# Digits for the second quarter of q and k, and three groups of transfers moved to SyncE, in a kernel of masked attention with an adjacency product

## The chip, the cores and the metric

The kernel runs on one core of a Trainium2 chip. The metric is device time in microseconds (us) of one execution; lower is better. The engines are named as in the profile: PE is TensorE, DVE is VectorE, ACT is ScalarE, POOL is GpSimd, SP is SyncE.

## What is computed

64 batches of 256 rows of 512 numbers pass two layers. Cut to what matters:

```
q = (x @ Wq + bq).reshape(b, n, 8, 64)          # k and v alike
scores = einsum('bqhd,bkhd->bhqk', q, k) / sqrt(64)
scores = scores + (1.0 - adj) * -1000000000.0
attn = softmax(scores)
out = einsum('bhqk,bkhd->bqhd', attn, v).reshape(b, n, 512) @ Wo + bo
x = layernorm(x + out)
y = einsum('nm,bmd->bnd', adj, x)
x = layernorm(x + y @ weight + bias)
```

## The kernel before

**Digits.** Plain fp32 products are slow on TensorE, so nearly all products are made of three products of shorter numbers (type fp32r). A number is cut into a high part (`split_high`, L118, ScalarE), a rest and a sum of both (`split_rest`, L123 and L124, two VectorE operations), and the rest is scaled (`split_scale`, L127, ScalarE). The names in the profile are high, low and diff (for x of the first pair sh, sl and sd; for weights the three buffers wr). `parts_of` (L334) issues for one block of 128 columns three groups of four matmuls (L339), in the order low, high, diff, or high, low, diff where `operands` (L331) says `soon`.

**Pairs and stages.** The batches are worked in 32 pairs p. A pair needs five sets of weights: qk0 (the first 256 columns of wq and wk), qk1 (the other 256), v, o and l. The list STAGES (L96) gives their order. Six buffers wr of 1 MB hold two stages. In the first pairs a stage is cut from the raw weights by `ring_high`, `ring_rest` and `ring_scale`, and `keep` (L129) stores its digits in DRAM by POOL's queue; later `load_w` (L105) brings them back by POOL's queue when `end_stage` is passed.

**The first pair is special.** The two quarters of q and of k that belong to qk0 (j = 0 and 1) are made in plain fp32 from the raw weights (L321, L322): four blocks, each of four fp32 matmuls that stand as eight rows in the profile. The first pair's first scores are therefore fp32 too. Stage qk0 is cut only later, for the second pair: `high` in `start` at L708 and L709, `rest` and `scale` at L713, after `scores(0, 1)`.

**Order.** `start` (L696), `first` (L646), `second` (L668) and `ending` (L720) write the order of work out by hand for TensorE, VectorE, ScalarE and POOL: within `tc.manual_schedule` (L764) these engines follow the source. SP is not among them: a planner orders its transfers. Each engine works its list in order, so an operation that waits holds all behind it. [...]

**Transfers by SP and POOL near the start.** SP loads x of the first pair, wq and wk in column parts (`load_columns`, L167), adj, wv, x of the second pair (`load_x`, L75, each of four transfers with runs of 128 B), bo and b1, and then x of the third pair as buffers come free. POOL stores the digits and loads wo (`load_o`, L208, called in L705). wo is used by `bv_wo` (L237) and when stage o is cut.

**Buffers that matter here.** Tile pools reuse buffers by name. The four buffers named low first hold x of the first pair and later x's low digits of the second (`x_rest`, L292); the four named diff hold its diff digits. `values` (L398) writes its sums into the one buffer zc (L413) and its products into the two buffers vc (L425), of which adj has one at first.

**The end.** `normed` (L530) normalizes a row block in place. For the last pair it issues the store at once: whole row blocks by SP, the last one in two halves, the first half by ScalarE and the second by SP (L543 to L545).

Of the kernel before, what the change touches and what calls it, by code (L numbers as in the profile page):

```python
# [8 lines left out]
F32 = mybir.dt.float32  # L9
F32R = mybir.dt.float32r  # L10
# [5 lines left out]
P = 128  # L16
# [19 lines left out]
def fast(tc, x, adj, wq, bq, wk, bk, wv, bv, wo, bo, w1, b1, out):  # L36
# [6 lines left out]
    nc = tc.nc  # L43
    B, N, D = x.shape
    HD = D // H
    DC = D // P
    NC = N // P
    NP = B // 2
    HF = D // 2
# [11 lines left out]
    one = pool("one", 1)  # L61
    two = pool("two", 2)
    four = pool("four", 4)
# [4 lines left out]
    banks = pool("banks", 8, space=bass.MemoryType.PSUM)  # L68

    XC, XF, XP, R, Q, K, V, E, SM, O, SET, HL, ST, LN = ({} for _ in range(14))  # L70
    RAW, SCRATCH, W, UNCUT, BEGUN = {}, {}, {}, {}, {}

    def load_x(p, i):  # L75

        if p < NP:

            t = XC[p, i] = two.tile([P, D], F32, name="o" if p == 1 and i > 1 else "x")
            for q in range(4):  # L80
                nc.sync.dma_start(t[q * 32:(q + 1) * 32].rearrange("i (m j) -> i m j", j=32), xb[p, i, q])
# [20 lines left out]
    def ring(name):  # L102
        return [wring.tile([P, 2, 2, D], F32R, name="wr") for _ in range(3)]
# [25 lines left out]
    def keep(name, i, part):  # L129

        SCRATCH[name, i] = scratch.tile([P, 2, 2, D], F32, name=f"{name}{i}")
        nc.gpsimd.dma_start(SCRATCH[name, i], part.bitcast(F32))

    def in_ring(f, name, p, k):

        stage = name, p
        if stage not in W:
            W[stage] = ring(name)
        t = [w[:, k // 2, k % 2] for w in W[stage]]
        if name in "vol":  # L140
            f(RAW[name, k], t)
        else:
            g, which = int(name[2]), "qk"[k // 2]
            raw = RAW[which][:, 2 * (k % 2):2 * (k % 2) + 2, g * HF:(g + 1) * HF]
            f(raw, [u.rearrange("p (k e) -> p k e", k=2) for u in t])
        if k == DC - 1 and f is not split_high:
            for i in (0, 2) if f is split_rest else (1,):
                keep(name, i, W[stage][i])

# [5 lines left out]

    def ring_scale(name, p, k):
        in_ring(split_scale, name, p, k)

# [33 lines left out]
    for k in range(DC):  # L194
        RAW["v", k] = four.tile([P, D], F32, name="high")
        nc.sync.dma_start(RAW["v", k], wv[k * P:(k + 1) * P])
    for i in range(4):
        load_x(1, i)
    bo_s, b1_s = on_all(bo, "bo"), on_all(b1, "b1")

    def small_ones():
# [2 lines left out]
        nc.gpsimd.memset(first_of_32, 0.0)  # L204
        for d in range(DC):
            nc.gpsimd.memset(first_of_32[d * 32:d * 32 + 1], 1.0)

    def load_o(k):  # L208
        if k % 2 == 0:
            RAW["o"] = two.tile([P, 2, D], F32, name="hl")  # L210
        RAW["o", k] = RAW["o"][:, k % 2]
        nc.gpsimd.dma_start(RAW["o", k], wo[k // 2 * HF:(k // 2 + 1) * HF].rearrange("(h a i) e -> a h i e", h=4, a=2)[k % 2])

    def load_l():
        t = two.tile([P, DC, D], F32, name="r")
# [98 lines left out]
    def operands(name, p, j, k):  # L314

        cols = slice(j * P, (j + 1) * P)
        if name == "v":
            pairs = [(XP[p, k][i][:, cols], W["v", p][i][:, k // 2, k % 2]) for i in range(3)]
        elif name in "qk":
            g, c = divmod(j, 2)  # L320
            if p == 0 and g == 0:  # L321
                return [(RAW[name][:, k, cols], XF[p, k])]  # L322
            e = slice(c * P, (c + 1) * P)
            w = [t[:, "qk".index(name)].rearrange("p s (k e) -> p (s k) e", k=2)[:, k, e] for t in W[f"qk{g}", p]]
            pairs = [(w[i], XP[p, k][i]) for i in range(3)]
        else:
            b, c = divmod(j, 2)
            t = SET[name, p, b, k // 2]
            pairs = [(t[i][:, k % 2, c * P:(c + 1) * P], W[name, min(p, NP - 2)][i][:, k // 2, k % 2]) for i in range(3)]

        soon = p == 1 and name in "qk" and j == 0 or p == NP - 1 and name in "ol"  # L331
        return [pairs[i] for i in ((0, 1, 2) if soon else (1, 0, 2))]

    def parts_of(pm, name, p, j, of=(0, 3)):  # L334
# [12 lines left out]
    def product(name, p, j):  # L347
        if (name, p, j) in BEGUN:
            pm = BEGUN.pop((name, p, j))
            n = parts_of(pm, name, p, j, (1, 3))  # L350
        else:
            pm = banks.tile([P, D], F32, name="ps")
            n = parts_of(pm, name, p, j)
        scale = RHO if n == 3 else 1.0
        b, c = divmod(j, 2)
        if name in "ol":
            r = R[p][b][:, c]
            if c == 0:
                ST[p, name, b] = two.tile([P, 2], F32, name="sums")
            nc.vector.scalar_tensor_tensor(r, pm, scale, r, op0=OP.mult, op1=OP.add, accum_out=ST[p, name, b][:, c:c + 1])  # L360
        elif name == "v":
            if c == 0:
                V[p, b] = two.tile([P, NC, D], F32, name="v")
            nc.scalar.activation(V[p, b][:, c], pm, AF.Copy, scale=scale)
        else:
            T, bias = (K, bk_s) if name == "k" else (Q, bq_s)
            if c == 0:
                T[p, b] = one.tile([P, 2, 3, D], F32R if n == 3 else F32, name=name + "T")
            if n == 3:
                to = UNCUT[name, p, j] = two.tile([P, D], F32, name="uncut")  # L370
            else:
                to = T[p, b][:, c, 0]
            nc.scalar.activation(to, pm, AF.Identity, bias=bias[:, j:j + 1], scale=scale)  # L373
# [112 lines left out]
    def masks(p, g, b):  # L486
        return [(masked, p, g, b, 0), (masked, p, g, b, 1), *([(summed, p, g, b)] if (p, g) != (NP - 1, 1) else [])]
# [145 lines left out]
    def do(*tasks):  # L633
        for t in tasks:
            for f, *args in (t if isinstance(t, list) else [t]):
                f(*args)
# [54 lines left out]
    def steps_of(*args):  # L691

        h, r, s = ([(f, *args, k) for k in range(4)] for f in (ring_high, ring_rest, ring_scale))
        return h[:2], r[:1] + h[2:3] + r[1:2] + h[3:], r[2:3] + s[:1] + r[3:] + s[1:2], s[2:]

    def start():  # L696
        make_identity(nc, ident)
        do(*((x_first, i) for i in range(4)), (biases,), *((x_high, 0, i) for i in range(4)), (small_ones,))
        qk1, v = (steps_of(*stage) for stage in STAGES[:2])
        high, rest, scale = ([(f, "qk0", 1, k) for k in range(DC)] for f in (ring_high, ring_rest, ring_scale))  # L700
        do((block, "q", 0, 0), (x_rest, 0, 0), (x_rest, 0, 1), qk1[0], (block, "k", 0, 0), (x_rest, 0, 2), (x_rest, 0, 3),
           qk1[1], (block, "q", 0, 1), qk1[2], v[0], (block, "k", 0, 1), v[1][:1], (x_t, 1, 0),
           (adj_t,), qk1[3])
        scores(0, 0)
        do(v[1][1:], (x_t, 1, 1), masks(0, 0, 0), (block, "q", 0, 2), v[2], *((load_o, k) for k in range(DC)), (qk_high, "q", 0, 2), (qk_rest, "q", 0, 2), v[3], (test_adj,),  # L705
           (block, "k", 0, 2), (x_high, 1, 0), (x_high, 1, 1), (qk_high, "k", 0, 2), (qk_rest, "k", 0, 2), masks(0, 0, 1),
           (block, "q", 0, 3), (k_low, 0, 2), (qk_high, "q", 0, 3), (qk_rest, "q", 0, 3), (x_rest, 1, 0), (x_t, 1, 2),
           (block, "k", 0, 3), (stage_end, 0), (qk_high, "k", 0, 3), (qk_rest, "k", 0, 3), (x_rest, 1, 1), (x_t, 1, 3), high[:2],  # L708
           (block, "v", 0, 0), (x_high, 1, 2), high[2:], (k_low, 0, 3), (block, "v", 0, 1), (x_rest, 1, 2),  # L709
           (block, "v", 0, 2), (x_high, 1, 3), (x_rest, 1, 3), (block, "v", 0, 3), (stage_end, 0), (load_r, 0), (load_l,))  # L710
        values(0, 0)
        scores(0, 1)
        do((bv_wo,), rest[:2], scale[:1], rest[2:3], scale[1:2], rest[3:], scale[2:])  # L713
        qk0 = [(f, name, 1, j) for j in range(2) for name in "qk" for f in (qk_high, qk_rest)]
        m = masks(0, 1, 0) + masks(0, 1, 1)
        do((begun, "q", 1, 0), (begun, "k", 1, 0), (block, "q", 1, 0), m[:4], qk0[:2], (block, "k", 1, 0), m[4:5], qk0[2:4], m[5:],
           (block, "q", 1, 1), (k_low, 1, 0), qk0[4:6], (o_high, 0, 0, 0), (o_high, 0, 1, 0), (o_rest, 0, 0, 0),
           (with_bv,), (block, "k", 1, 1), qk0[6:], (stage_end, 0), (k_low, 1, 1), (o_rest, 0, 1, 0))
# [42 lines left out]
           (last_variance,), (root, 1), (less, p, "l", 1, c1), (normed, p, "l", 3, D // 2))  # L761

    PE, DVE, ACT, POOL = mybir.EngineType.PE, mybir.EngineType.DVE, mybir.EngineType.Activation, mybir.EngineType.Pool
    with tc.manual_schedule(engines={PE, DVE, ACT, POOL}):  # L764
        start()
        first(1, steps_of("o", 0))
        second(1)
        load_r(1)
        for w in range(2, NP - 1):
            first(w)  # L770
            second(w)
        ending()

    good = one.tile([P, 2, N // 32], F32, name="z")
# [186 lines left out]
```

## Time and profile before

| what | before |
|---|---|
| median of 3 runs | 2391.67 us (2391.25 to 2391.77) |
| the profiled execution: device time | 2391.06 us |
| its span (first to last instruction) | 2389.2 us |
| granted TensorE clock, mean | 0.999 |
| PE / DVE / ACT / POOL busy | 2374.3 / 1991.0 / 1505.4 / 443.5 us |
| DMA moved | 608.70 MB, mean 255 GB/s |
| PE busy from 8 to 22 us (x of first pair, q and k in fp32) | 13.92 us |
| PE busy from 69 to 77 us | 7.54 us |
| DMA share from 37 to 48 us | 1.09 of the 16 engines |

The page gives busy time by engine, the granted clock and DMA share in 40 slices, the chain that ended last and the costliest groups. A row of the timeline has start, length, engine, line, operation and tiles, output before input. A TensorE row's end is modelled, so durations of matmuls are read from one start to the next. The profiled execution has its own time; a sum of rows is made against it and then carried over to the median of the runs.

### The profile page before, as it was taken

How to read it: one execution, taken by the hardware profiler on the slowest of the kernel's cores; microseconds unless marked ns; L12 is line 12 of the kernel's file. 1: busy time of each engine (PE TensorE's matmuls, PEld its weight loads, DVE VectorE, ACT ScalarE, POOL GpSimd, SP SyncE). 2: the span in 40 equal slices, each digit the busy share in tenths (PEclk: the TensorE clock that was granted, in tenths of full speed). 3: DMA queues.
4: the chain of work that ended last, by engine and by line, in shares of the span. 5: the costliest groups of instructions: out<-in, count | busy, mean ns of one | idle time of the engine just before them, and what ended most of it. 6: DMA issues, size and time to landing. Idle time of an engine off the chain costs nothing.

```text
span 2389.2 us, 43002 instructions
## 1 busy us (share of the span) xinstructions
PE 2374.3 (99%) x16925; PEld 1907.5 (80%) x16925; DVE 1991.0 (83%) x3311; ACT 1505.4 (63%) x2793; POOL 443.5 (19%) x755
## 2 busy tenths in 40 slices
PE   9999999999999999999999999999999999999998
PEld 6788887888878888878888788887888878888776
DVE  7988888888888888888988888888888888888867
ACT  6666666566565665666656656666566665666655
POOL 1222111111111111121111112111111111121121
PEclk9999999999999999999999999999999999999999
DMA  9897788777888777887777967788778887777782
GB/s 295 274 310 244 265 255 283 259 230 256 260 265 271 241 237 256 264 293 238 236 255 254 310 240 224 265 255 286 258 227 261 261 264 268 238 244 255 256 274 62
DMA packets 373651, 608.70 MB, mean 255 GB/s; under 512 B 272316, under 2 KB 275908, under 8 KB 313156
## 3 DMA queue, kind: packets, MB, share of 16 engines
q0 software_dynamic: 71632, 500.21, 57.5%
q1 hardware_dynamic: 301104, 105.29, 20.4%
q8 instruction: 135, 2.21, 0.4%
q14 instruction: 72, 0.59, 0.1%
q10 hardware_dynamic: 708, 0.40, 0.1%
HBM read 551.29 MB, written 49.28 MB: 251 GB/s over the span
## 4 chain that ended last, share of the span: by engine, by line
PE 96%; DVE 1%; ACT 0%; issue 0%; POOLq 0%; ACTq 0%
PE ps L339 72%; PE ps L421 9%; PE ps L455 8%; PE ps L615 5%; PE ps L411 3%; DVE e L476 0%; DVE wr L124 0%; DVE wr L123 0%; PE ps L565 0%; DVE kT L389 0%; DVE qT L387 0%; DVE qT L385 0%; ACT kT L394 0%; DVE kT L385 0%; ACT waste L517 0%
## 5 line engine op out<-in xcount | busy, mean ns | idle before, releaser
L373 ACT ACTIVATE uncut<-ps,numbers 128x512 f32<-128x512 f32 x252 | 174.0, 690 | 274.0 <-PE ps L339 218.1
L476 DVE TENSOR_TENSOR e<-e,adjT 128x1024 f32<-128x1024 f32 x252 | 299.3, 1219 | 0.2 <-ACT e L470 0.2
L339 PE MATMUL ps<-low,wr 128*128 128x512 f32 x992 | 271.6, 395 | 0.0
L339 PE MATMUL ps<-wr,sl 128*128 128x512 f32 x1008 | 270.6, 390 | 0.1
L339 PE MATMUL ps<-wr,sh 128*128 128x512 f32 x1008 | 269.8, 389 | 0.0
L339 PE MATMUL ps<-wr,sd 128*128 128x512 f32 x1008 | 269.4, 389 | 0.0
L339 PE MATMUL ps<-high,wr 128*128 128x512 f32 x992 | 266.4, 390 | 0.0
L339 PE MATMUL ps<-diff,wr 128*128 128x512 f32 x992 | 265.0, 389 | 0.0
L523 POOL TENSOR_TENSOR ln<-ln,numbers 128x2 f32<-128x2 f32 x127 | 140.4, 1105 | 667.0 <-DVE ln L522 621.3
L470 ACT ACTIVATE e<-ps 128x512 f32<-128x512 f32 x504 | 253.3, 629 | 8.6 <-PE ps L455 8.6
L517 ACT ACTIVATE waste<-r,ln 128x512 bf16<-128x512 f32 x255 | 184.0, 722 | 104.6 <-DVE ln L510 98.9
L421 PE MATMUL ps<-e,v 128*32 128x256 f32 x4032 | 229.1, 379 | 0.0
L538 ACT ACTIVATE r<-r,ln 128x512 f32<-128x512 f32 x254 | 193.7, 811 | 55.1 <-DMA x<-in_x_dram 29.9
L339 PEld LDWEIGHTS ps<-wr,sh 128*128 128x128 f32 x1008 | 189.3, 188 | 39.9
L339 PEld LDWEIGHTS ps<-wr,sd 128*128 128x128 f32 x1008 | 189.2, 188 | 39.5 <-DMA wr<-o 0.2
L339 PEld LDWEIGHTS ps<-high,wr 128*128 128x128 f32 x992 | 186.2, 188 | 41.9 <-ACT e L470 0.8
L339 PEld LDWEIGHTS ps<-diff,wr 128*128 128x128 f32 x992 | 186.2, 188 | 39.1
L339 PEld LDWEIGHTS ps<-wr,sl 128*128 128x128 f32 x1008 | 186.9, 188 | 38.2 <-issue 0.4
L455 PEld LDWEIGHTS ps<-qT,kT 64*128 64x128 f32 x3056 | 187.8, 187 | 27.1 <-PE ps L421 12.4
L385 DVE SCALAR_TENSOR_TENSOR qT<-qT,uncut 128x512 fp32r<-128x512 f32 x126 | 86.8, 689 | 146.9 <-ACT qT L378 146.8
L339 PEld LDWEIGHTS ps<-low,wr 128*128 128x128 f32 x992 | 177.7, 188 | 35.5 <-ACT wr L127 0.6
L455 PE MATMUL ps<-qT,kT 64*128 64x256 f32 x3056 | 201.6, 285 | 0.5 <-ACT kT L394 0.5
(166 smaller groups left out, 4156.1 us busy)
## 6 DMA issues: line engine op xcount, KB each, us to landing
wr<-qk POOLq DMA_DIRECT2D x183, 1024.0 KB, 7.6
wr<-v POOLq DMA_DIRECT2D x93, 1024.0 KB, 6.8
wr<-o POOLq DMA_DIRECT2D x90, 1024.0 KB, 7.8
wr<-l POOLq DMA_DIRECT2D x90, 1024.0 KB, 8.6
r<-in_x_dram SPq DMA_DIRECT2D x32, 1024.0 KB, 12.0
out_dram<-r SPq DMA_DIRECT2D x62, 512.0 KB, 2.9
x<-in_x_dram SPq DMA_DIRECT2D x488, 64.0 KB, 5.4
qk<-wr POOLq DMA_DIRECT2D x6, 1024.0 KB, 8.3
```

The source lines that it names most:

```text
L339: nc.tensor.matmul(pm, *pairs[k][i], start=i == 0 and k == 0, stop=i == n - 1 and k == DC - 1)
L373: nc.scalar.activation(to, pm, AF.Identity, bias=bias[:, j:j + 1], scale=scale)
L385: nc.vector.scalar_tensor_tensor(low, high.bitcast(F32), -RHO, UNCUT.pop((name, p, j)), op0=OP.mult, op1=OP.add)
L411: nc.tensor.matmul(at[h * 32:(h + 1) * 32, b, :], ones, chunk[h], start=i == 0, stop=i == len(sm) - 1)
L421: nc.tensor.matmul(at[h * 32:(h + 1) * 32, a, :], V[p, b][:, kc, col:col + 32], E[p, g, b, kc][0][h % 2][:, h // 2, :], start=kc == 0, sto ...
L455: nc.tensor.matmul(sc[s][:, a, :], K[p, g][r, a, i, keys], Q[p, g][r, a, i, b * N:(b + 1) * N], start=i == digits[0], stop=i == digits[-1])
L470: nc.scalar.activation(e[s], sc[s], AF.Exp, scale=(RHO if (p, g) != (0, 0) else 1.0) * qscale)
L476: nc.vector.tensor_tensor(e, e, mask[:, kc:kc + 1, :].to_broadcast([P, e.shape[1], N]), op=OP.mult)
L517: nc.scalar.activation(waste, R[p][b][:, c], AF.Square, bias=t[0][:, c:c + 1], accum_out=t[1][:, c:c + 1])
L523: nc.gpsimd.tensor_tensor(t[2], t[1], power[:, cs], op=OP.pow)
L538: nc.scalar.activation(r[:, :cut], r[:, :cut], AF.Identity, scale=scale, bias=bias)
L615: nc.tensor.matmul(pm[:, j, :], t[:, i, mc, j * P:(j + 1) * P], adjT[:, mc, :], start=mc == 0 and i == 0, stop=mc == NC - 1 and i == 1)
```

## The change

1. The digits of columns 128 to 255 of wq and wk are cut first of all, into buffers that are otherwise free at that time (`cut`, with low, diff, zc and vc as room), and the first pair's blocks q and k with j = 1 use them instead of plain fp32. The results of these blocks still go to the fp32 buffers of the first scores.
2. For the second pair, stage qk0 takes this half by six SBUF-to-SBUF transfers on SP (`cut_over`), and only the other half (columns 0 to 127) is cut afresh, in two steps instead of four: high between the products of `values(0, 0)`, rest and scale after `scores(0, 1)`, now ahead of `bv_wo`.
3. wo is loaded by SP, between the second pair's first and last two x loads, instead of by POOL.
4. `keep` stores the digits of o and l by SP instead of POOL.
5. In `ending`, SP follows the source as well.
6. Around this the order of `start` is rewritten: qk1 is cut before the first k block, the transposes of the second pair's x and the first masks change places.

The diff, cut to its core:

```diff
-        nc.gpsimd.dma_start(SCRATCH[name, i], part.bitcast(F32))
+        (nc.sync if name in "ol" else nc.gpsimd).dma_start(SCRATCH[name, i], part.bitcast(F32))
...
+        elif name == "qk0":
+
+            t = [w[:, k].rearrange("p s (k e) -> p (s k) e", k=2)[:, :, :P] for w in W[stage]]
+            f(RAW["qk"[k]][:, :, :P], t)
...
-        if k == DC - 1 and f is not split_high:
+        if k == (1 if name == "qk0" else DC - 1) and f is not split_high:
...
+    def cut(f, k):
+        if (k, 0) not in EARLY:
+            for i in range(3):
+                pool_of, name = ((four, "low"), (four, "diff"), (one, "zc"), (two, "vc"))[k + (2 if i == 2 else 0)]
+                EARLY[k, i] = pool_of.tile([P, DC, P], F32R, name=name)
+        f(RAW["qk"[k]][:, :, P:2 * P], [EARLY[k, i] for i in range(3)])
...
+    def cut_over():
+        W["qk0", 1] = ring("qk0")
+        for i, t in enumerate(W["qk0", 1]):
+            for k in range(2):
+                to = t[:, k].rearrange("p s (k e) -> p (s k) e", k=2)[:, :, P:2 * P]
+                nc.sync.dma_start(to.bitcast(F32), EARLY[k, i].bitcast(F32))
...
-    for i in range(4):
+    for i in range(2):
+        load_x(1, i)
+    for k in range(DC):
+        if k % 2 == 0:
+            RAW["o"] = two.tile([P, 2, D], F32, name="hl")
+        RAW["o", k] = RAW["o"][:, k % 2]
+        nc.sync.dma_start(RAW["o", k], wo[k // 2 * HF:(k // 2 + 1) * HF].rearrange("(h a i) e -> a h i e", h=4, a=2)[k % 2])
+    for i in range(2, 4):
         load_x(1, i)
...
-            if p == 0 and g == 0:
+            if p == 0 and j == 0:
                 return [(RAW[name][:, k, cols], XF[p, k])]
             e = slice(c * P, (c + 1) * P)
-            w = [t[:, "qk".index(name)].rearrange("p s (k e) -> p (s k) e", k=2)[:, k, e] for t in W[f"qk{g}", p]]
+            if p == 0 and g == 0:
+                w = [EARLY["qk".index(name), i][:, k] for i in range(3)]
+            else:
+                w = [t[:, "qk".index(name)].rearrange("p s (k e) -> p (s k) e", k=2)[:, k, e] for t in W[f"qk{g}", p]]
...
-        soon = p == 1 and name in "qk" and j == 0 or p == NP - 1 and name in "ol"
+        soon = name in "qk" and (p, j) in ((0, 1), (1, 0)) or p == NP - 1 and name in "ol"
...
-        do((block, "q", 0, 0), (x_rest, 0, 0), (x_rest, 0, 1), qk1[0], (block, "k", 0, 0), (x_rest, 0, 2), (x_rest, 0, 3),
-           qk1[1], (block, "q", 0, 1), qk1[2], v[0], (block, "k", 0, 1), v[1][:1], (x_t, 1, 0),
-           (adj_t,), qk1[3])
+        do((cut_high, 0), (cut_high, 1), (block, "q", 0, 0), (x_rest, 0, 0), (x_rest, 0, 1), (x_rest, 0, 2), (cut_rest, 0), (x_rest, 0, 3),
+           (cut_rest, 1), h, (cut_scale, 0), (block, "k", 0, 0), (cut_scale, 1), r[:2],
+           (block, "q", 0, 1), c[:2], r[2:], (block, "k", 0, 1), v[0], v[1][:1], (adj_t,), c[2:])
         scores(0, 0)
-        do(v[1][1:], (x_t, 1, 1), masks(0, 0, 0), (block, "q", 0, 2), v[2], *((load_o, k) for k in range(DC)), (qk_high, "q", 0, 2), (qk_rest, "q", 0, 2), v[3], (test_adj,),
+        do(v[1][1:2], masks(0, 0, 0), (x_t, 1, 0), v[1][2:], (x_t, 1, 1), (block, "q", 0, 2), v[2], (qk_high, "q", 0, 2), (qk_rest, "q", 0, 2), v[3], (test_adj,),
...
-           (block, "k", 0, 3), (stage_end, 0), (qk_high, "k", 0, 3), (qk_rest, "k", 0, 3), (x_rest, 1, 1), (x_t, 1, 3), high[:2],
-           (block, "v", 0, 0), (x_high, 1, 2), high[2:], (k_low, 0, 3), (block, "v", 0, 1), (x_rest, 1, 2),
+           (block, "k", 0, 3), (stage_end, 0), (cut_over,), (qk_high, "k", 0, 3), (qk_rest, "k", 0, 3), (x_rest, 1, 1), (x_t, 1, 3),
+           (block, "v", 0, 0), (x_high, 1, 2), (k_low, 0, 3), (block, "v", 0, 1), (x_rest, 1, 2),
...
-        values(0, 0)
+        values(0, 0, (high[:1], high[1:]))
         scores(0, 1)
-        do((bv_wo,), rest[:2], scale[:1], rest[2:3], scale[1:2], rest[3:], scale[2:])
+        do(rest, scale, (bv_wo,))
...
-        ending()
+    with tc.manual_schedule(engines={PE, DVE, ACT, POOL, SP}):
+        ending()
```

`h`, `r` and `c` are the high, rest and scale steps of qk1; `high`, `rest` and `scale` are now lists of two, for q and for k.

More of the change, by code (lines that the diff above doesn't have):

```diff
@@ L70, in fast @@
     XC, XF, XP, R, Q, K, V, E, SM, O, SET, HL, ST, LN = ({} for _ in range(14))
-    RAW, SCRATCH, W, UNCUT, BEGUN = {}, {}, {}, {}, {}
+    RAW, SCRATCH, W, UNCUT, BEGUN, EARLY = {}, {}, {}, {}, {}, {}
     def load_x(p, i):
@@ L157, in ring_scale, with cut_high, cut_rest, cut_scale @@
         in_ring(split_scale, name, p, k)
+    def cut(f, k):
[4 more added lines that the diff above has]
+        f(RAW["qk"[k]][:, :, P:2 * P], [EARLY[k, i] for i in range(3)])
+    def cut_high(k):
+        cut(split_high, k)
+    def cut_rest(k):
+        cut(split_rest, k)
+    def cut_scale(k):
+        cut(split_scale, k)
+    def cut_over():
[4 more added lines that the diff above has]
+                nc.sync.dma_start(to.bitcast(F32), EARLY[k, i].bitcast(F32))
     ones = cpool.tile([P, 32], F32, name="ones")
@@ L206, in small_ones @@
             nc.gpsimd.memset(first_of_32[d * 32:d * 32 + 1], 1.0)
[L208 to L212, printed above, removed]
     def load_l():
@@ L366, in product @@
             T, bias = (K, bk_s) if name == "k" else (Q, bq_s)
+            digits = (p, b) != (0, 0)
             if c == 0:
-                T[p, b] = one.tile([P, 2, 3, D], F32R if n == 3 else F32, name=name + "T")
-            if n == 3:
+                T[p, b] = one.tile([P, 2, 3, D], F32R if digits else F32, name=name + "T")
+            if digits:
                 to = UNCUT[name, p, j] = two.tile([P, D], F32, name="uncut")
@@ L698, in start @@
         do(*((x_first, i) for i in range(4)), (biases,), *((x_high, 0, i) for i in range(4)), (small_ones,))
-        qk1, v = (steps_of(*stage) for stage in STAGES[:2])
-        high, rest, scale = ([(f, "qk0", 1, k) for k in range(DC)] for f in (ring_high, ring_rest, ring_scale))
-        do((block, "q", 0, 0), (x_rest, 0, 0), (x_rest, 0, 1), qk1[0], (block, "k", 0, 0), (x_rest, 0, 2), (x_rest, 0, 3),
-           qk1[1], (block, "q", 0, 1), qk1[2], v[0], (block, "k", 0, 1), v[1][:1], (x_t, 1, 0),
-           (adj_t,), qk1[3])
+        h, r, c = ([(f, "qk1", 0, k) for k in range(DC)] for f in (ring_high, ring_rest, ring_scale))
@@ L704, in start @@
+        v = steps_of("v", 0)
+        high, rest, scale = ([(f, "qk0", 1, k) for k in range(2)] for f in (ring_high, ring_rest, ring_scale))
+        do((cut_high, 0), (cut_high, 1), (block, "q", 0, 0), (x_rest, 0, 0), (x_rest, 0, 1), (x_rest, 0, 2), (cut_rest, 0), (x_rest, 0, 3),
+           (cut_rest, 1), h, (cut_scale, 0), (block, "k", 0, 0), (cut_scale, 1), r[:2],
+           (block, "q", 0, 1), c[:2], r[2:], (block, "k", 0, 1), v[0], v[1][:1], (adj_t,), c[2:])
         scores(0, 0)
-        do(v[1][1:], (x_t, 1, 1), masks(0, 0, 0), (block, "q", 0, 2), v[2], *((load_o, k) for k in range(DC)), (qk_high, "q", 0, 2), (qk_rest, "q", 0, 2), v[3], (test_adj,),
+        do(v[1][1:2], masks(0, 0, 0), (x_t, 1, 0), v[1][2:], (x_t, 1, 1), (block, "q", 0, 2), v[2], (qk_high, "q", 0, 2), (qk_rest, "q", 0, 2), v[3], (test_adj,),
@@ L763, in fast @@
     PE, DVE, ACT, POOL = mybir.EngineType.PE, mybir.EngineType.DVE, mybir.EngineType.Activation, mybir.EngineType.Pool
+    SP = mybir.EngineType.SP
     with tc.manual_schedule(engines={PE, DVE, ACT, POOL}):
```

## The prediction, made before the changed kernel was run

> **What bounds the kernel now.** I read the page first (shares, then the chain that ended last), then TensorE's waits, then TensorE's timeline and the chain over the first 110 us (all that the change touches but its tail lies there), then the DMA view, then the end.
>
> ```profile
> PE 2374.3 (99%) x16925; PEld 1907.5 (80%) x16925; DVE 1991.0 (83%) x3311; ACT 1505.4 (63%) x2793; POOL 443.5 (19%) x755
> ...
> PE 96%; DVE 1%; ACT 0%; issue 0%; POOLq 0%; ACTq 0%
> ```
>
> TensorE is busy for 2374.3 of 2389.2 us and makes 96% of the chain. Its waits are few:
>
> ```profile
> PE ps L261 <- DMA low<-in_x_dram: 4.1, 2, 3.8
> PE ps L455 <- ACT kT L394: 0.5, 1, 0.5
> PE ps L271 <- issue: 0.2, 1, 0.2
> ```
>
> So from 8.2 us to the last product only one wait, of 0.5 us, is seen. Whatever shortens TensorE's queue before 77 us shortens the whole, one for one; whatever eases only DMA, POOL or SP gives nothing.
>
> ```profile
> 8.18 14.00 PE L339 MATMUL ps<-e,r 128*128 128x512 f32 x32
> 22.01 0.60 PE L228 MATMUL ps<-z,vc 128*128 128x128 f32 x4
> ...
> 26.20 1.19 PE L339 MATMUL ps<-sl,wr 128*128 128x512 f32 x4
> 27.23 1.08 PE L339 MATMUL ps<-sh,wr 128*128 128x512 f32 x4
> 28.15 1.07 PE L339 MATMUL ps<-sd,wr 128*128 128x512 f32 x4
> 29.05 1.07 PE L339 MATMUL ps<-sl,wr 128*128 128x512 f32 x4
> ...
> 56.70 2.09 PE L339 MATMUL ps<-high,wr 128*128 128x512 f32 x8
> 58.74 1.24 PE L339 MATMUL ps<-low,wr 128*128 128x512 f32 x4
> 59.82 1.09 PE L339 MATMUL ps<-diff,wr 128*128 128x512 f32 x4
> ...
> 74.54 2.76 PE L455 MATMUL ps<-qT,kT 64*128 64x256 f32 x42 [0.46 <-ACT kT L394]
> ```
>
> (Start, length, then the group.) Four blocks in plain fp32 start at 8.18 and the next work at 22.01: 13.83/4 = 3.46 us a block. Blocks of digits advance by 0.91 us for each four matmuls, 12 matmuls 2.72 us. The chain says who made the wait at 74.54:
>
> ```profile
> 54.79 0.69 DVE wr L124
> ...
> 72.50 0.61 DVE kT L385
> 73.13 0.70 DVE kT L389
> 73.86 0.64 ACT kT L394
> 74.54 2.76 PE ps L455 x42
> ```
>
> VectorE is in the chain almost without a gap from 54.8 to 73.8 us, beginning with the eight digit operations of stage qk0 (L123, L124).
>
> [...] 13.83/16 = 0.86 us for an fp32 matmul against 0.227, 3.8 times. [...] here the share of the 16 engines is 1.03 to 1.27 in every stretch from 8 to 69 us. [...] eight SP transfers of only 64 KB wait behind POOL's of 1 MB, with a median of 16.3 us to landing for those issued from 34 to 48 us.
>
> **The change, part by part.**
>
> *q and k, second quarter, in digits.* Two fp32 blocks go (2 x 3.46 = 6.92 us), two of digits come (2 x 2.72 = 5.44), and one more entry from fp32 into digits (the first four after the scores took 27.23 - 26.20 = 1.03 instead of 0.91): -6.92 + 5.44 + 0.12 = **-1.36 us**, on the path. Do the digits come in time? ScalarE ends its four x_high at 10.5, the two cut_high end at 11.6 (0.55 each). VectorE starts at 8.95 and a rest (two operations) takes 1.33: x 0, 1, 2, then cut q until 14.3, x 3 until 15.6, cut k until 16.9. The q block starts at 15.2 with the high digits (order 0, 1, 2), needs the scaled low of q at 16.1 (ScalarE: after four ring_high, about 15.3) and the diff at 17.0 (14.3; x 3's 15.6). k's low is needed at 18.8 (16.9), its diff at 19.7 (16.9). Cover 0.8 us at the least; no wait taken.
>
> *After these blocks.* VectorE did two rests more, so the copy to adjT ends at 24.2 (23.6 before) while TensorE is 1.4 earlier; the scores' eighth bank can be adj_t's, wanted at about 24.1. I take **+0.1**; bounds 0 and +0.7 (the whole lateness). ScalarE's exps begin at about 23.6 (23.8 before), the banks of q's third block are free by then.
>
> *qk0: half split afresh, half copied.* VectorE loses four of the eight operations at 54 to 59.4, -2.66 us, and ScalarE two high and two scale (-2.1); the same amount was added before 17 us. By my count VectorE ends x_rest(1, 3) at 49.7 (48.7 before), zc is ready at 48.9, o at 52.7, rests end at 55.3: the masks start at 55.3 instead of 59.4, 4.1 us earlier, while TensorE is 1.4 earlier. The chain into k_low then ends about 2 us ahead of the scores, so the 0.46 wait goes: **-0.46**. What is late next is TensorE itself. The low digits at 58.74 waited for ScalarE's scales (57.97 to 60.24): four took 1.08 instead of 0.91, and the eight before them 2.04 instead of 1.81 of which 0.12 is the entry. Scales now end at 57.1: **-0.2** (bounds 0, -0.3).
>
> *The six copies on SP* (cut_over, 256 KB each in runs of 512 B). They wait for the third stage's k block (35.8 now), and SP reaches them at about 36.4: wo's four issues (0.47 each, L196's median) and x(2, 0) stand before. Price: the k and q columns have the same form and took 4.4 us to landing alone; all six are 1.57 MB, at the 303 GB/s of 5 to 10 us 5.2 us. Beside them: the last of v's stores (2.6 us for 1 MB) and what is left of x(2, 0) (about 1). Landed by 36.4 + 5.2 + 2.6 + 1 = 45.2, estimate; from 43 (alone) to 54.3 (the fourth's issue at 38.0 + 16.3). Who waits: x_rest(1, 2) on VectorE for low and diff at 47.1; ScalarE's zc at 48.3; vc at 51.3; TensorE for q's second block at 60. Cover 1.9 us or more: **0**. Behind them on SP: x(2, 1), used at 75 us, 20 us of cover.
>
> *wo on SP* is moved past x(1, 2), x(1, 3), bo, b1 and x(2, 0), each about 2 us later; x(1, 3) landed at 32.3 and is transposed at 45.5, so 0. It leaves POOL ahead of v's last store, and DMA a stretch in which it moved slowly (13.0 us to landing). It is read by bv_wo at 54 us. **0**.
>
> *Stores of o and l on SP*: 6 x 0.55 us leave POOL; behind them stood loads into the ring that wait for TensorE anyway. On SP o's (ready 91.4 to 96.6) fall between x loads issued until 90.2 and from 104.7; l's (ready 121.6 to 126.6) hold the load of r from 122.9 to about 127, and r is first used at 164.5. **0**.
>
> ```profile
> hl<-in_L_gnn_Wo_dram POOLq DMA_DIRECT2D x4, 256.0 KB, 13.0
> ...
> r<-in_L_gnn_Wk_dram SPq DMA_DIRECT2D x2, 256.0 KB, 4.4
> ```
>
> *The last stores.* SP's queue had the last quarter row (ready 2381.7) ahead of the third row (ready 2381.0), whose store was then issued at 2382.1 and landed at 2385.4. In order of source the third row goes at 2381.0, and the 128 KB one is last. That ends SP's waits some 0.5 to 1.2 us sooner. But:
>
> ```profile
> L956 POOLq DRAIN x3: 46/107/6479, 2381.6 to 2388.9; - x3
> L956 SPq DRAIN x3: 7/7/7, 2386.6 to 2388.3; - x3
> ```
>
> POOL's longest drain runs from 2381.6 to 2388.1, past SP's 2386.7, so SP seems not the last. Bounds 0 and -1.2; taken **-0.2**.
>
> **Sum**: -1.36 + 0.1 - 0.46 - 0.2 - 0.2 = -2.1 us. The profiled execution took 2391.06 (span 2389.2 and 1.9 around it) and becomes 2388.95; the median of the runs, 2391.67, lies 0.6 above it: 2391.67 - 2.1 = **2389.6 us**, 0.09% less. About 0.2% (4.8 us) is what a measurement of this kernel can tell from no change, so this counts as the same.
>
> **Rivals.** (1) *Part is given back* (0.2): VectorE, 1 us later than before at 49 us, or adj_t's bank makes a wait of up to 0.7 and the scale's 0.2 stays: -1.2, 2390.5. For it: VectorE's idle time from 15 to 49 us was 2.0 us (1.4 and 0.6 in its waits), and most of it is now spent. Against: what TensorE takes from it there is due at 35 and later. (2) *Copies land late, slower* (0.1): if SP's 512 B packets starve behind POOL's as the 64 KB loads did, x_rest(1, 2) waits until 54.3 instead of 47.1; VectorE's masks then start at 62.5, 3.1 after before's 59.4, the chain into k_low with them, and TensorE stalls at the scores until 77.6: +3.1, 2394.8. It decides from a landing at 47.1 + 4.1 = 51.2 us. Against: wo has left that stretch, and v's next loads wait for the end of the v blocks. (3) *The tail pays in full* (0.1): -1 more, 2388.5. (4) The forecast, 0.6. That the digits are not used is no rival: q's and k's second blocks read EARLY in the code.
>
> **Numbers.** The range reaches from the tail's full pay with the rest's upper bounds, 2388.3, to a gain of only 0.3, 2391.4; the late copies (0.1) and half of their neighbours are left out. Faster by over 0.2% needs -4.8, more than all bounds together (0.01); slower by over 0.2% is a landing at 56 us or later (0.03).
>
> **What would show it.** TensorE's timeline: fp32 products 16 instead of 32 from 8.18, two blocks of digits from 15.2, adj_t near 20.7; no wait before 77 us; scores of the second pair of batches at about 71.4 instead of 73.45. VectorE's masks of the first pair's second half at 55.3 instead of 59.4. SP's copies landed before 47. If VectorE or ScalarE is released by one of SP's copies, (2) is true. The pieces after 77 us should keep their lengths; if they change, the argument from TensorE's unbroken queue is wrong.

## The result, and the profile after

The changed kernel is slower: 2405.14 us (median of 6 runs, 2404.22 to 2406.82) against 2391.37 us of the kernel before in the same measurement. The ratio is 1.0056, 95% interval 1.0045 to 1.0067. The forecast was 2389.6 with a range from 2388.3 to 2391.4. The profiled execution took 2405.45 us with a span of 2403.5.

The page's shares and the chain of what ended last, of the changed kernel:

```profile
PE 2378.6 (99%) x16933; PEld 1911.3 (80%) x16933; DVE 1990.6 (83%) x3311; ACT 1502.1 (62%) x2793; POOL 436.5 (18%) x745
...
PE 96%; SPq 2%; DMA 1%; ACT 0%; DVE 0%; issue 0%; POOLq 0%; ACTq 0%
```

The shares hardly tell the two kernels apart. What is new in the chain is SP's queue with 2%, where there was none. TensorE's waits (us in total, times, longest), in the first 130 us:

```profile
PE ps L455 <- ACT v L397: 9.6, 2, 5.0
...
PE ps L489 <- ACT zc L447: 1.1, 1, 1.1
PE ps L489 <- ACT vc L459: 0.6, 1, 0.6
PE ps L372 <- ACT wr L127: 0.4, 1, 0.4
```

TensorE now waits for V of the first pair, for zc and vc, and for scaled digits of stage qk0 (wr). Where it does so, its timeline shows (start, length, group, wait ahead of it):

```profile
8.54 7.23 PE L372 MATMUL ps<-e,r 128*128 128x512 f32 x16 [0.27 <-ACT e L295]
15.20 1.49 PE L372 MATMUL ps<-sh,low 128*128 128x512 f32 x4
16.53 1.09 PE L372 MATMUL ps<-sl,low 128*128 128x512 f32 x4
...
21.14 0.60 PE L258 MATMUL ps<-z,vc 128*128 128x128 f32 x4
...
47.72 1.07 PE L445 MATMUL ps<-sm,ones 128*32 128x256 f32 x16
...
54.19 3.64 PE L455 MATMUL ps<-e,v 128*32 128x256 f32 x32 [4.97 <-ACT v L397]
62.48 2.79 PE L455 MATMUL ps<-e,v 128*32 128x256 f32 x24 [4.65 <-ACT v L397]
...
68.80 1.39 PE L489 MATMUL ps<-qT,kT 64*128 64x256 f32 x12 [1.10 <-ACT zc L447]
...
92.98 1.19 PE L372 MATMUL ps<-wr,low 128*128 128x512 f32 x4
```

Until 47.72 us the change does what it was meant to: 16 rows of fp32 products instead of 32, then digits (from 15.20), and the blocks of V end half a us earlier than before (47.72 against 48.18). All the loss lies between 48 and 72 us. The same cut, from group start to group start, for the two kernels and for the best one of the experiments (wo in eight transfers and POOL's loads of v later, below); each column adds up to its span:

| stretch of TensorE's queue, us | before | changed | best | forecast of the difference |
|---|---|---|---|---|
| start to the first fp32 product | 8.18 | 8.54 | 8.66 | 0 |
| fp32 and digits, up to adj_t | 13.83 | 12.60 | 12.91 | -1.36 |
| adj_t to the first sums (sm,ones) | 26.17 | 26.58 | 26.54 | +0.1 |
| first sums to the second pair's blocks (wr,low) | 29.05 | 45.26 | 28.03 | -0.66 |
| from there to the start of TensorE's last group | 2301.78 | 2301.73 | 2301.67 | 0 |
| start of TensorE's last group to the end of the span | 10.19 | 8.79 | 8.69 | -0.2 |

The fourth row has the whole loss, +16.2 us. Who made it, the chain over 24 to 95 us says (start, length, what):

```profile
23.02 1.41 SPq L232
...
24.48 10.29 SPq L81
...
34.82 8.16 SPq L81
...
46.71 13.11 DMA o<-in_x_dram
```

SP issues the last of wo's four loads (L232) at 23.02 and then needs 10.29 us to issue one x load of 64 KB (L81), and 8.16 for the next; before, the longest of these eight took 1.72 us. One part of x(1, 3) lands at 59.8 us, the start of its transposition is at 60.57, and the engines that follow wait one behind the other. ScalarE's x_high (L315) waits for VectorE's transpose (L307), and that for x:

```profile
50.98 0.71 DVE L307 STREAM_TRANSPOSE xT<-o 128x512 f32<-128x512 f32 x1 [6.64 <-DMA o<-in_x_dram]
```

ScalarE's queue holds the copies of V behind x_high: x_high waits 10.66 us until 51.73, the first two of the copies follow at 53.56. So TensorE waits for V, although nothing of V needs this x. SP's six copies (L186), issued from 60.95 us instead of the expected 36.4, are late too: that is the wait for zc.

The waits in that stretch make 4.97 + 4.65 + 1.10 + 0.62 + 0.41 = 11.75 us, 11.3 more than the 0.46 before; the loss is 16.2. Most of the rest is clock. Two stretches of the changed kernel (window, length, busy time and instructions of PE, PEld, DVE, ACT and POOL, then the granted TensorE clock, DMA share and GB/s):

```profile
48.00:54.00 6.00, 1.22 (x24) 0.48 (x16) 2.95 (x5) 1.61 (x3) 0.54 (x1) 0.93 1.04 376
54.00:58.00 4.00, 3.64 (x32) 1.38 (x32) 0.32 (x1) 0.63 (x2) 0.00 (x0) 0.50 1.32 296
```

After a pause of 5 us the products run at half clock, 0.50 from 54 to 66 us and 0.80 from 66 to 68, where the kernel before has 1.00 from 54 to 66: 32 products of e and v took 3.64 us, as long as 64 take in the kernel before. The three groups from 54.19 to 67.7 us lose some 4.1 of the remaining 4.9 us so: without their waits they took 3.64, 2.72 and 2.50 us, and the same work takes 1.79, 1.34 and 1.60 in the kernel before. The prediction's rivals priced a wait at its own length.

### The profile page after: what moved, and what is told of

Same layout as the page of the kernel before. It is cut to its first block, busy times and chain, and to the rows that moved or that the text cites. A ratio compares the mean times of both kernels' runs of the same rounds, so it can differ in the third digit from the quotient of the medians.

```text
span 2403.5 us, 43029 instructions
## 1 busy us (share of the span) xinstructions
PE 2378.6 (99%) x16933; PEld 1911.3 (80%) x16933; DVE 1990.6 (83%) x3311; ACT 1502.1 (62%) x2793; POOL 436.5 (18%) x745
## 4 chain that ended last, share of the span: by engine, by line
PE 96%; SPq 2%; DMA 1%; ACT 0%; DVE 0%; issue 0%; POOLq 0%; ACTq 0%
PE ps L372 72%; PE ps L455 9%; PE ps L489 8%; PE ps L649 5%; PE ps L445 3%; SPq L81 1%; DMA o<-in_x_dram 1%; DMA vc<-in_adj_dram 0%; DMA low<-in_x_dram 0%; DMA wr<-zc 0%; ACT e L504 0%; SPq L232 0%; SPq L186 0%; PE ps L599 0%; SPq L198 0%
## 5 line engine op out<-in xcount | busy, mean ns | idle before, releaser
L455 PEld LDWEIGHTS ps<-e,v 128*32 128x32 f32 x4032 | 131.6, 111 | 98.6 <-ACT v L397 11.0
```

The lines of the kernel that those rows point to most:

```text
L455: nc.tensor.matmul(at[h * 32:(h + 1) * 32, a, :], V[p, b][:, kc, col:col + 32], E[p, g, b, kc][0][h % 2][:, h // 2, :], start=kc == 0, sto ...
```

## The experiments

Each run was measured beside the kernel before on the same chip, where that took 2391.8 us (medians 2391.77 to 2391.85). The theories A to D are stated with the first run; A was mine.

### wo back to POOL, and wo alone to SP

The first is the changed kernel with one thing undone:

```diff
-    for k in range(DC):
...
-        nc.sync.dma_start(RAW["o", k], wo[k // 2 * HF:(k // 2 + 1) * HF].rearrange("(h a i) e -> a h i e", h=4, a=2)[k % 2])
...
+        do(v[1][1:2], ..., (block, "q", 0, 2), v[2], *((load_o, k) for k in range(DC)), (qk_high, "q", 0, 2), ...
```

> The changed kernel with one thing undone: wo is loaded by POOL again, at its old place in the order; digits, copies, SyncE's stores and last stores stay. Theory A (wo's four loads on SP run on few DMA engines and block the x loads queued behind them): the whole loss goes, x(1,2) and x(1,3) land before 40 us, PE's waits for v and zc between 48 and 72 us vanish, time 2389.6 (2388.3 to 2391.4, the forecast). Theory B (wo's bytes ahead of x in SP's queue, however many engines carry them): the same, 2389.6. Theory C (the copies of the digits, or the stores that now come close together, crowd the x loads out): still about 2405. Theory D (the new order of VectorE's and ScalarE's steps): still about 2405.

Measured: 2391.32 us, ratio 1.0000 (0.9992 to 1.0009). No wait for v; TensorE waits 0.6 for vc and 0.4 for the scales. The 13 us are gone; the gain that A's 2389.6 stood for is not seen.

The second is the kernel before with only that edit done, the other way round.

> The kernel before with one thing done: wo's four loads go from POOL to SyncE, between x(1,1) and x(1,2). Theories A and B: most of the loss comes with it alone, 10 to 16 us over the kernel before (2401 to 2407), with the long waits of PE for v between 50 and 75 us. Theories C and D: no change, 2391.4 within 1.

Measured: 2404.36 us, ratio 1.0055 (1.0041 to 1.0068); TensorE waits 11.7 us for v. So wo's move alone carries a loss of this size, and C and D fall as its cause: the kernel of the first run has the copies and the new order and loses nothing. This does not show that the copies are free.

### Few engines, or bytes

Four loads of 128 rows become sixteen of 32, same place, same bytes, same packets:

```diff
-        nc.sync.dma_start(RAW["o", k], wo[k // 2 * HF:(k // 2 + 1) * HF].rearrange("(h a i) e -> a h i e", h=4, a=2)[k % 2])
+        for h in range(4):
+            r = k // 2 * HF + h * 64 + k % 2 * 32
+            nc.sync.dma_start(RAW["o", k][h * 32:(h + 1) * 32], wo[r:r + 32])
```

In the kernel before with wo on SP:

> The kernel before with wo on SyncE between x(1,1) and x(1,2), as in the run that was 13 us slower, but with each of the four transfers cut into four of 32 rows. There are no copies of digits here that could be late. Theory A (four engines): x(1,2) and x(1,3) land before 46 us as they did in the changed kernel with the cut loads, no wait for v, 2391.4 within 1. Theory B (bytes and places in the queue): 2400 or more.

Measured: 2390.49 us, ratio 0.9995 (0.9987 to 1.0004), against 1.0055 uncut. x(1, 2) and x(1, 3) in the DMA views from 20 to 60 us, with wo uncut (first) and cut (issues, KB each, median us to landing; 5.3 in the kernel before):

```profile
o<-in_x_dram SPq DMA_DIRECT2D x8, 64.0 KB, 18.2
```

```profile
o<-in_x_dram SPq DMA_DIRECT2D x8, 64.0 KB, 7.7
```

Only the cut of wo's transfers differs (their slowest dimension, and with it their number and size), and it is worth 13.9 us: A holds for the x loads, B falls. Size alone is not the cause: wv's loads by SP are 256 KB each too, and in the kernel before they took 0.43 to 0.63 us to issue and 6.6 to 7.9 us to landing. From 13 to 14 us of that kernel, where SP's queue is alone and 179 of its 235 packets are wv's (those of 2 KB), it takes 104.4% of the 16 engines and moves 398 GB/s. wo's source runs over h = 4 slowest, wv's over 128 rows, the cut loads' over 32. The DMA view of the changed kernel from 44.6 to 46 us, where POOL's queue is all but empty (queue, packets, MB, share of 16 engines):

```profile
q1 hardware_dynamic: 71, 0.14, 26.0%
q0 software_dynamic: 3, 0.00, 0.1%
```

SP's packets are of 2 KB here, which are wo's (x comes in runs of 128 B). They take as much as 0.26 x 16 = 4.2 engines and move 101 GB/s, while x waits behind them. How many engines the cut loads used is not shown, nor what in wo's pattern keeps its share so low; shown are 26.0% for wo, 104.4% for wv, and x's landing in 7.7 us instead of 18.2 once wo is cut. By POOL in the kernel before, wo with the same pattern landed in 13.0 us.

The same cut in the changed kernel:

> The changed kernel with wo still on SyncE and at the same place in its queue, but each of the four transfers cut into four of 32 rows, so that the source's slowest dimension is 32 and not 4: the same bytes in the same packets of 2048 B. Theory A (few engines): [...] x(1,2) lands before 40 us, 2389.6 to 2391.5. Theory B (bytes ahead of x in the queue): x stays late, above 2400. Theories C and D: about 2405.

Measured: 2401.19 us, ratio 1.0041 (1.0027 to 1.0054). A was wrong for this kernel as a whole. The waits for v are gone, and another took their place:

```profile
PE ps L491 <- ACT zc L449: 8.0, 1, 8.0
```

ScalarE waits 12.0 us for a copy of digits to leave zc. With x in time, the copies are the victim.

### Where wo stands in SP's queue

wo uncut, behind x(1, 2) and x(1, 3) (the second loop of `load_x` moved ahead of wo's):

> The changed kernel with wo's four loads on SyncE, uncut, moved behind x(1,2) and x(1,3) in the queue. Theory A: x in time, so the 10 us of waits for v go; what is queued behind wo now (bo, b1, x(2,0) and the six copies of digits) stands behind the same few engines, so the copies may land some us late: 2389.6 if they land by 51 us, up to 2395 if not. Theory B: the same. Theories C and D: about 2405.

Measured: 2404.72 us, ratio 1.0052 (1.0038 to 1.0066). x is in time, no wait for v; but behind wo now stand bo (9.42 us to issue), x(2, 0) (14.74 for four) and the copies, issued at 58.05 to 63.32 instead of 36. TensorE waits 12.1 us for zc. A's mechanism holds, its size (up to 2395) was far off: the delay goes on to whatever is next.

wo uncut, behind the copies:

```diff
-           ... (stage_end, 0), (cut_over,), (qk_high, "k", 0, 3), ...
+           ... (stage_end, 0), (cut_over,), *((load_o, k) for k in range(DC)), (qk_high, "k", 0, 3), ...   # load_o by SP
```

> The changed kernel with wo's four loads on SyncE, uncut, moved behind the six copies of digits in its queue (issued after the copies, ahead of x(2,1), r and w1). Theory A (whatever stands behind wo's four loads in SyncE's queue comes late, and nothing else in the change costs): x(1,3) lands before 36 us, the copies are issued from about 33 us and land by 48, sooner than with wo on POOL (51 to 53.5), because POOL moves nothing but its v stores then; x(2,1), r and w1 come up to 20 us later, which nobody waits for; 2389.5 (2388.3 to 2391). Theory E (the copies are the cost wherever wo stands, because they cross POOL's own transfers): PE still waits for zc or vc, several us, 2393 or more. Theory F (what now comes behind wo, r, w1 and x(2,1), is needed in time): a new wait after 70 us, 2393 or more.

Measured: 2409.82 us, ratio 1.0078 (1.0064 to 1.0091): the slowest of all, and none of the three theories had it. x and the copies are in time (the copies, issued from 35.6 us, take 5.4 to 6.8 us), so E falls. It is wo itself that is late:

```profile
PE ps L272 <- DMA hl<-in_L_gnn_Wo_dram: 14.9, 3, 10.2
```

`bv_wo` reads wo from 55.7 us on. Issued at 43.4 to 46.6, the last of it is used at 74.6; that is 1 MB in 31 us, some 34 GB/s. That is a third of the 101 GB/s above. This run shows wo's own deadline and speed; it doesn't tell A from B.

### The copies, and POOL's loads of v

wo in eight transfers of 64 rows, so that SP is through with it sooner:

```diff
...
+        for h in range(4):
+            r = c * HF + h * 64
+            nc.sync.dma_start(RAW["o"][h * 32:(h + 1) * 32], wo[r:r + 64].rearrange("(a i) e -> i a e", a=2))
...
```

> The changed kernel with wo on SyncE at the same place, but as eight transfers of 64 rows (slowest dimension 32, 128 KB each): half as many issues as the sixteen that gave 2401. Theory G (two things in wo's move cost: the four engines, and what wo takes of SyncE's queue ahead of the copies, which then meet POOL's v loads): wo's issues take about 6 us instead of 11.2, the copies are issued from about 40 us instead of 45 and most of them land before POOL's v loads crowd them; PE's wait for zc falls from 8.0 us to 0 to 4, time 2391 to 2396. Rival H (the crowding by POOL's loads decides, not when the copies are issued): the wait for zc stays at 7 us or more, 2400.

Measured: 2399.86 us, ratio 1.0033 (1.0020 to 1.0045), 7.7 us of waiting for zc. Rival H holds. wo's issues took 6.0 us instead of 11.2, but the eight x loads behind wo took 11.0 instead of 6.8, so the copies went out only at 43.3 to 48.4. POOL's timeline has the first of three loads of v's digits beside them, the others 0.9 and 1.8 us behind:

```profile
46.28 0.55 POOL L110 DMA_DIRECT2D wr<-v  x1 [10.86 <-PE ps L374]
```

In the kernel before the first of these three loads came at 36.95, the two others only at 50.10:

```profile
50.10 1.08 POOL L110 DMA_DIRECT2D wr<-v  x2 [12.59 <-DMA v<-wr]
```

There they waited for a store of v's digits that stood behind wo in POOL's queue. With wo gone they wait only for the buffers that V's blocks leave, and so those two come 2 to 3 us sooner, and all three into the copies; in the changed kernel with wo on POOL all three came at 51.92. The DMA view of this run from 49 to 57 us (queue, packets, MB, share of 16 engines):

```profile
q0 software_dynamic: 376, 2.82, 90.1%
q1 hardware_dynamic: 490, 0.25, 13.9%
```

POOL's queue (q0) sent 376 packets and SP's (q1) 490, the same order. But POOL's are 7.5 KB each and took 0.901 x 16 x 8 us / 376 = 0.31 us, SP's 0.5 KB and 0.036 us. So SP's queue moves 0.25 MB, 31 GB/s, beside the 2.82 MB of POOL's.

The test: this kernel with one more edit, POOL's loads of v 7 us later:

```diff
-           ... (block, "v", 0, 3), (stage_end, 0), (load_r, 0), (load_l,))
+           ... (block, "v", 0, 3), (load_r, 0), (load_l,))
...
-        do(rest, scale, (bv_wo,))
+        do((stage_end, 0), rest, scale, (bv_wo,))
```

> The run before last of the changed kernel, wo in eight transfers (2399.9, PE waits 7.7 us for zc), with one more edit: the call that brings v's digits back for the second pair (three loads of 1 MB by POOL, issued there at 46.3 to 48.1, while the copies were under way) stands behind the second scores instead of behind the v blocks, and so some 10 us later. Theory I (POOL's loads of v, which come 5 us sooner once wo has left POOL's queue, crowd the copies' small packets out): all copies land before 53, the wait for zc falls to 0 to 1 us, about 2391 (2389.5 to 2392.5). Rival J (the copies are slow whatever runs beside them, or SyncE issues them too late): the wait stays above 4 us, 2396 or more. Rival K (v's digits come too late for the second pair): a new wait behind 77 us.

Measured: **2388.37 us, ratio 0.9986 (0.9979 to 0.9992)**: faster than the kernel before and than the changed one. The copies are issued at the same times (43.77 to 47.84), zc's has landed at 50.45, and POOL's loads follow at 53.19. TensorE's waits of this run, all of them:

```profile
PE ps L293 <- DMA low<-in_x_dram: 4.3, 2, 3.9
PE ps L374 <- ACT e L297: 0.3, 1, 0.3
```

The DMA view from 46 to 50 us, with nothing of POOL's in it:

```profile
q1 hardware_dynamic: 2684, 1.33, 114.5%
...
wr<-zc SPq DMA_DIRECT2D x1, 256.0 KB, 3.3
```

SP's queue moves 333 GB/s instead of 31, and zc's copy lands in 3.3 us instead of 13.8. I holds, J and K fall. ScalarE still waits 0.7 us for zc's copy, so no cover is left there.

### The other parts by themselves

The digits and their copies alone (wo and the stores by POOL, SP's last stores unordered):

> The changed kernel without what it does to SyncE's other work: wo loaded by POOL at its old place, stores of o's and l's digits by POOL, SyncE's last stores in the order of before; only the digits of the second quarter and their copies stay. Forecast: -1.36 at the projections and -0.5 at the scores less 0.6 to 1.0 that PE now waits for vc and wr: 2390.0 to 2391.0 against 2391.4. Rival (the copies eat the gain): 2391.4 or more.

Measured: 2392.84 us, ratio 1.0007 (0.9998 to 1.0015), the rival's side if any. The products up to adj_t took 12.96 us (13.83 before), the first scores gave back 0.4, and TensorE waits 0.6 for vc and 0.4 for the scales, as the copies land beside POOL's wo. The stretch from the first sums to the second pair's blocks took 30.4 us (29.05 before), so in this profile the stretch in which the copies are awaited lost more than the digits gave. The interval does not tell the time from no change.

Stores and last stores alone:

> The kernel before with only the stores of o's and l's digits moved to SyncE and SyncE's last stores put into the order of the source. Forecast: -0.2 (0 to -1.2), all of it behind the last product: from PE's last instruction to the end of the span 10.2 us before, 9 to 10 here; 2390.2 to 2391.4. Rival (SyncE in the written order makes a store wait): the stretch behind the last product is longer than 10.2 us.

Measured: 2390.85 us, ratio 0.9997 (0.9989 to 1.0006); behind TensorE's last instruction 9.4 us instead of 10.2. This with wo in sixteen transfers on SP, without digits:

> The kernel before with everything of the change but the digits: wo on SyncE (cut into sixteen transfers[...]), stores of o's and l's digits by SyncE, SyncE's last stores in the order of the source. The two gains of the single runs added: -0.9 for the end, and 0 to -1.3 for wo: 2389.6 to 2391.0 against 2391.8 of the kernel before on that chip. Rival (they overlap or one of them was chance): 2391.0 or more.

Measured: 2390.21 us, ratio 0.9995 (0.9986 to 1.0003). The times of both allow a gain of about 1 us and also none. Over all profiles the stretch behind the last instruction is 8.6 to 10.3 us in the four with the old order of stores (mean 9.5) and 8.1 to 9.4 in the ten with the new (mean 8.8), so the gain is about 0.7 us, inside the scatter.

The digits without the copies (no `cut_over`, all of stage qk0 cut afresh as before; wo in eight transfers, stores and end as changed):

> The changed kernel with the early digits used for the first pair only: no copies by SyncE, the whole of stage qk0 is cut afresh after the scores as in the kernel before; wo on SyncE in eight transfers, stores and end as changed. Theory G (copies and wo's engines are the whole loss): no wait for zc or vc, about 2390. What the copies were for: VectorE's four operations at 54 to 59 us are back, so PE's wait for k at the scores, 0.5 us in the kernel before, grows by the 1.3 us that PE now comes earlier, to 1.5 to 2.0, and the digits' gain is gone; with the end's -0.9 this makes 2390.0 to 2391.2. Rival (VectorE catches up, the wait stays 0.5): 2388.5 to 2389.5. Theories C and D (the copies are not needed for a loss, the new order is): 2400 or more.

Measured: 2389.43 us, ratio 0.9990 (0.9983 to 0.9996), faster than before. C and D fall once more. I had expected the digits' gain to be gone; the time lies in the rival's range, since TensorE's wait at the scores grows less than I thought:

```profile
PE ps L478 <- ACT kT L417: 0.7, 1, 0.7
```

The digits' gain was mostly kept. With the copies, and POOL's loads of v put off for them, it is about 1 us more (2388.37 against 2389.43); the two runs differ in both edits.

## Why the prediction was wrong

**The step that failed** is "wo on SP", priced at 0 with the words "each about 2 us later". It counted four issues of 0.47 us, what an issue of a wv load took. But a wv load runs over 128 rows, wo's over four groups, and wo almost alone took only 26.0% of the 16 engines, at 101 GB/s. x(1, 3), expected by some 34 us, landed at up to 59.8, 14 us past its use at 45.5; the cover that the step named was real, and too small by that. The two runs that differ in the cut alone (2404.36 and 2390.49) show that the form of wo's transfers is the cause. The step also counted as a benefit that wo "leaves POOL ahead of v's last store": that is what let POOL's loads of v come at 46.3 us into the copies, and where x is in time it costs 11.5 us (2399.86 against 2388.37 with those loads put off).

**The six copies**, priced at 0 with a landing at 45.2: SP reached them at 60.95 instead of 36.4 for the same cause. Where SP was free (wo behind them) they were issued from 35.6 and took 5.4 to 6.8 us each, about what was forecast. The argument against rival (2), that v's next loads wait for the end of the V blocks, was right on when they come (46.3), but it holds only for copies issued at 36; with x in time and wo still ahead of them they went out at 43.3 or later. The view from 34 to 48 us on which the price of 16.3 us rests shows four transfers, not eight.

**Rival (2)** had the mechanism of the copies and its sign, with a chance of 0.1 and 3.1 us. Its decision point, a landing past 51.2 us, fits: with wo on POOL the copies landed at 51.3 to 53.5, and TensorE waited 0.6 us for vc and 0.4 for the scales; with zc's landed at 60.9 it waited 7.7 for zc. The stretch from the first sums shows more than these waits: 29.9 and 38.8 us, against 28.0 in the best kernel. Its price lacked the half clock after a pause (0.50 from 58 to 66 us with wo in eight transfers).

**Digits, -1.36**: right in kind, too large in size. The two digit blocks took 5.94 us (15.20 to 21.14) in the changed kernel and 5.90 in the best, where 5.44 + 0.12 = 5.56 were forecast. The 0.12 for the entry was read behind the scores; behind plain fp32 the first four matmuls took 1.33 us instead of 0.91. Against two fp32 blocks of 6.92 us this leaves -1.0. The table's -1.2 and -0.9 hold also what the 16 rows of fp32 ahead did: 6.66 us in the changed kernel, 7.01 in the best, and 8.58 in the run with wo in sixteen transfers. The first of these rows starts at 8.1 to 8.2 us in the two kernels with neither digits nor wo on SP, and at 8.5 to 9.0 in all others; no step foresaw that, and its cause is not shown. No wait for digits came.

**adj_t's bank, +0.1 (0 to 0.7)**: +0.4 in every kernel with digits; the first scores take 4.10 us instead of 3.73. That the bank is the reason is not shown. **The waits at the scores and scales, -0.66**: -1.0 in the best kernel, where the wait of 0.46 is gone as forecast. **Stores of o and l, 0**: no wait for them is seen. **The last stores, -0.2 (0 to -1.2)**: some -0.7, not settled.

With both of SP's troubles taken away by two edits that the prediction did not have, the medians give 3.4 us less than the kernel before (2.7 by the two profiles), where 2.1 were predicted. That the sums lie so near is in part chance: by the table the digits and the first scores gave 0.7 less than forecast and the start lost 0.5, while the tail gave 1.3 more, which is inside its scatter.

What stays open: what in wo's pattern kept its share at 26.0%, how many engines the cut transfers used, and why SP needs 17 to 18 us to issue the cut wo and the eight x loads together, in eight transfers as in sixteen. The loss of the changed kernel can't be divided between x and the copies, since there the first hides the second: x late alone cost 12.5 us (2404.36 in the kernel before with wo on SP), the copies late alone 9.3 (2401.19 with wo cut), each against the kernel before.

## What to carry to other kernels

Before a transfer is moved to another queue, compare its access patterns with those of a transfer already timed there, not its size alone, and count what stands behind it: here loads that took 26.0% of the 16 engines delayed what followed in their queue (x landed in 18.2 us, and in 7.7 with the loads cut), and slowed even its issues (10.29 us for one of 64 KB, at most 1.72 before). Ask of every transfer that leaves a queue what it was holding back there: here 0.5 KB packets that met 7.5 KB packets went out in about the same number (490 and 376), and so carried a small part of the bytes (0.25 MB beside 2.82). If small copies must run near large loads, keep them apart in time: here that was worth 11.5 us (2399.86 against 2388.37). Two ways kept the copies in time here: issued at 35.6 us, ahead of wo, or POOL's loads of v 7 us later. The copies 1.7 us sooner (43.3 instead of 45.0, with wo in eight transfers instead of sixteen) hardly helped: 2399.86 against 2401.19.

## What the runs showed of the hardware that was not expected

- Four loads of a pattern with 4 as its slowest dimension took 26.0% of the 16 engines while they ran almost alone, at 101 GB/s; in a stretch mostly of loads with 128 there it was 104.4%, at 398 GB/s.
- Issuing one DMA of 64 KB right behind these loads took SP 10.29 us, and 12.58 in the run with wo behind the copies; in the kernel before the same eight x loads took 0.64 to 1.72 us each.
- TensorE's pauses cost more than their length: 11.3 us of added waits became 16.2 us, mostly because the clock was 0.50 from 54 to 66 us.
- The same copies took 3.1 to 3.3 us to landing alone, 5.4 to 6.8 where they were issued from 35.6 us ahead of wo, 11.2 to 14.6 beside POOL's wo and 13.8 (zc's) beside its loads of v (as far as their landings are seen).
- Right behind plain fp32 the first four matmuls in digits took 1.33 us, the next four 0.92.
